# Around the first block's MLP: earlier rows, later weight groups, other buffers for the second down step

## The chip, the cores and the metric

The kernel runs on one core of a Trainium2 chip. Its time is the device time of one execution in microseconds (us), the median of several runs. Engines are named as in the profile: PE (matrix engine), DVE (vector), ACT (scalar), POOL (GpSimd) and SP, whose queue issues the DMAs.

## The reference, cut to what matters

Two transformer blocks run one after the other on 16 sequences of 256 tokens with 512 channels, in fp32. The first block is cross attention to a context, a residual, a layer norm and an MLP with a hidden size of 2048:

```python
out = jnp.einsum('bhnm,bmhd->bnhd', attn, v).reshape(B, N, C)
out = out @ proj_w + proj_b
x = x + out
h = layer_norm(x, n2_w, n2_b)
h = jax.nn.gelu(h @ fc1_w + fc1_b, approximate=False) @ fc2_w + fc2_b
return x + h
```

The second block is causal self attention, cross attention and a small MLP, each with a residual and a layer norm. The change touches the first block's MLP and the end of the attention ahead of it.

## The kernel before, in words

**Precision.** A product of fp32 matrices is made of three matmuls in a faster format: each operand is split into a rounded part and the rest (tiles called `_h` and `_l`, or `x_t` and `c_t`). ACT writes the rounded part, DVE subtracts it to get the rest (`split_lazy`, L141 and L142). POOL does this for the first weights ("early").

**Tiling.** The 4096 rows are 8 batches g of 512 rows (NG = 8, four tiles of 128 rows each). The MLP (class `Mlp0`) runs 32 up steps (fc1 and gelu) and then 32 down steps (fc2): four for each batch, each over two of the eight weight groups of 256 hidden columns. A step is a 2 x 2 block product in seven products instead of eight (a Strassen form): four sums of blocks are made first (`differences`, L802 to L805, for the values, and L851 to L854 in `weigh`, for the weights), and the seven results are added up by DVE. Each product is 12 matmuls of 128 x 128 by 128 x 256, so a step is 84 matmuls.

**Up step** (`up`, PE line L914). Products go in the order 1, 6, 5, 2, 7 with the last two (4, 3) of a step inside the step that follows. `L945` (u2 = p1 + the bank of product 6) and `L970` (u3 = p1 + the bank after product 7) must have read the PSUM bank called "sc" before PE may go on in it. Gelu is on ACT (L979). The gelu'd tile `ho` is stored to DRAM (`hid`, L953). Weights of fc1 are loaded by `fetch` (L818), split and combined by `weigh`; two groups m = 2s, 2s + 1 serve step s of every batch. `begin` loads and prepares the first two groups and the first batch's rows while the attention of the last batch is still running; `open` the next two; `run` weighs groups 4 and 5 after the first up step has been recorded, 6 and 7 after the second.

**Entry.** `last` in `phase1` fills PE's gaps in the attention of the last batch: values, the projection of attention outputs with its residual (`residual`: a row of x is loaded at L671, POOL adds a bias at L672, DVE adds the product at L685, and it is stored at L686), and `Mlp0.begin`. `begin` loads 512 rows `xn` (L870), of which DVE takes the statistics (`bn_stats`, L238) and the normalized value (L247). The attention itself uses all engines: scores on PE (L408), their minimum with the mask on DVE (L423), exp on ACT (L433), transposes (L449) that ACT or DVE copies out (L455, L453), products with the values (L468), and the scaling by reciprocals of sums (L627 on DVE, L629 on POOL, L644 on PE, L647, L136 and L137 on DVE).

**Down step** (`down`, PE line L1027). `hidden(n)` loads the stored values of step n (L993, 1 MB), `sums_down(n)` makes their four sums, `write` splits the seven operands into the slots that PE reads, one after each product of the step before. Products go in the order 1, 6, 2, 7, 5, 4, 3. Weights of fc2 are fetched and weighed during the last four up steps, the last two groups (6 and 7) during the first two down steps. After the four steps of a batch, `end` and `finish` add up the results and the residual rows x (loaded at L1039, POOL adds a bias at L1044) on DVE.

**Buffers.** Big tiles share tags with one buffer each: "raw", "x0", "x1", "x2" (1 MB each in the on-chip memory). A tile of a tag waits until the last reader of the one before it is done. Before the change, `hidden` uses "raw" for even steps and "x0" for odd ones, and the sums of every step but the first are in "x2". In the last up steps "x0" holds weights (fetched at L818 for the last steps), and "x2" holds the gelu'd tile of even up steps.

**Order.** PE's order is the order in which the code records it (`tc.manual_schedule` for PE). The order on ACT, DVE, POOL and SP is made by a scheduler of the framework that runs a timing model of its own; each engine then works strictly in that order, waiting on semaphores.

The functions that the change touches, with the line numbers of the profile:

Of the kernel before, what the change touches and what calls it, by code (L numbers as in the profile page):

```python
# [41 lines left out]
def kernel(ctx: ExitStack, tc: tile.TileContext, a, out):  # L42
# [511 lines left out]
    def phase1():  # L554
# [184 lines left out]
        def last():  # L739
            yield from more_values(NG - 1)  # L740
            right.close()
            mlp = w["mlp"] = Mlp0()
            mlp.small = pool, 4
            yield from residual(NG - 2, 1)
            yield from mlp.begin()
            yield from residual(NG - 1, 0)
            xrs = [residual_row(NG - 1, NT)]
            yield from turned(NG * NB)
            top.close()
            xrs.append(residual_row(NG - 1, NT + 1, mlp.open()))  # L750
            yield from residual(NG - 1, 1, xrs)
# [9 lines left out]
    class Mlp0:  # L761
# [163 lines left out]
        def up(self, n, between):  # L925


            s = n % self.NS if n < NG * self.NS else None
            on, after = s is not None, n > 0
            add = nc.vector.tensor_tensor  # L930
            if on:
                self.product_up(n, 1, "mm", True)
                first = self.flat("p1")
                nc.scalar.copy(first, self.banks[n, "mm"])
            else:
                between[0]()
            if after:
                p1, u2, ho = self.open
                self.product_up(n - 1, 4, "sc", False)
                add(ho[:, :, 0, self.W :], p1, self.banks.pop((n - 1, "sc")), ALU.add)  # L940
                self.gelu(n - 1, ho, 0, slice(self.W, N))
            if on:
                self.product_up(n, 6, "sc", True)
                v2 = self.flat("u2")
                add(v2, first, self.banks[n, "sc"], ALU.add)  # L945
            else:
                between[1]()
            if after:
                self.product_up(n - 1, 3, "pt", False)
                add(ho[:, :, 1, : self.W], u2, self.banks.pop((n - 1, "pt")), ALU.add)  # L950
                self.gelu(n - 1, ho, 1, slice(0, N))
                g, q = divmod(n - 1, self.NS)
                nc.sync.dma_start(  # L953
                    out=self.hid[g][q], in_=ho.rearrange("p m c n -> p (m c n)")
                )
            if not on:
                return
            self.product_up(n, 5, "pt", True)
            between[0]()
            self.product_up(n, 2, "mm", False)  # L960
            if n % 2 == 0:
                ho = self.px.tile([P, 2, 2, N], F32, tag="x2", name="ho")
            else:
                ho = self.up_pool.tile([P, 2, 2, N], F32, tag="ho", name="ho", bufs=1)
            x = self.banks.pop((n, "mm"))
            for mm in range(2):
                self.gelu(n, ho, 0, slice(0, self.W), x[:, mm, :], mm)
            self.product_up(n, 7, "sc", False)
            u3 = self.flat("u3")
            add(u3, first, self.banks[n, "sc"], ALU.add)  # L970
            add(ho[:, :, 1, self.W :], u3, self.banks[n, "pt"], ALU.add)
            between[1]()
            self.open = first, v2, ho
# [15 lines left out]

        def hidden(self, n):  # L990
            g, q = self.order(n)
            h = self.raw_tile("x0" if n % 2 else "raw").rearrange("p (m c n) -> p m c n", m=2, c=2)
            nc.sync.dma_start(out=h.rearrange("p m c n -> p (m c n)"), in_=self.hid[g][q])  # L993
            self.h[n] = h

        def sums_down(self, n):
            h = self.h.pop(n)
            b = [[h[:, :, k, ts(t, self.W)] for k in range(2)] for t in range(2)]
            if n == 0:

                s = [self.place("sums") for _ in range(2)]
                two = self.tmp.tile([P, 4, 2 * P], F32, tag="diff", name="sums")
                two = two.rearrange("p (i m) n -> p i m n", m=2)
                s = [x.rearrange("p (m n) -> p m n", m=2) for x in s] + [two[:, i] for i in range(2)]
            else:
                s = self.px.tile([P, 4, 2, self.W], F32, tag="x2", name="sums")
                s = [s[:, i] for i in range(4)]
            self.differences(b[1][0], b[1][1], b[0][0], b[0][1], s, nc.vector, nc.vector)
            self.a = [b[0][0], b[0][1], b[1][1]] + s
# [26 lines left out]
        def residual(self, g):  # L1036
            x = self.px.tile([P, G, C], F32, tag="x1", name="x")
            for t in range(G):
                nc.sync.dma_start(out=x[:, t, :], in_=xd[0][g][ts(t, P), :])  # L1039
            return x  # L1040
# [46 lines left out]
        def begin(self):  # L1087


            self.fetch(1, 0, self.raw_tile("raw"))  # L1090
            xn = self.px.tile([P, G, C], F32, tag="x2", name="xn")
            for t in range(G):
                self.row(0, t, xn[:, t, :])
            self.fetch(1, 1, self.raw_tile("x1"))
            yield 12 * PASS
            for t in range(G):
                self.normal(xn[:, t, :])
                yield 3 * PASS
            for m in range(2):
                self.weigh(1, m, True)  # L1100
                yield 12 * PASS
            for t in range(G):
                yield self.turn(0, t, xn[:, t, :])
            self.sums(True)
            for i in range(7):
                self.write(i, nc.gpsimd)
# [20 lines left out]
        def run(self, early, after_up):  # L1127

            for m in range(self.NM - 1, 3, -1):
                self.open_group(m)  # L1130
            left = ExitStack()
            self.up_pool = sbuf(left, "work2", 1)
            xn = self.xn
            last = NG * self.NS - 1

            def load(g):

                if g > 1:
                    x = self.pool.tile([P, G, C], F32, tag="raw", name="xn")
                    for t in range(G):  # L1140
                        xn[t] = self.row(g, t, x[:, t, :])

            def go(g, t):
                self.turn(g, t, xn.pop(t))
                if g == 1 and t == 0:
                    xn[G - 1] = self.row(g, G - 1, self.place())
                if t == G - 1:
                    self.sums()

            for n in range(last + 1):  # L1150
                g, s = divmod(n, self.NS)
                between = [lambda: None, lambda: None]
                if g + 1 < NG:
                    if s == 0:
                        load(g + 1)
                    elif s <= 2:
                        for t in (2 * s - 2, 2 * s - 1) if g else ():
                            self.normal(xn[t])
                        between = [lambda t=2 * s - 2 + i: go(g + 1, t) for i in range(2)]
                elif s == self.NS - 1:  # L1160
                    self.sums_down(0)
                self.up(n, between)
                if n == 0:
                    self.weigh(1, 4)
                    self.weigh(1, 5)
                    self.fetch(1, 3, self.raw_tile("raw"))
                elif n == 1:
                    self.weigh(1, 6)
                    self.normal(xn[G - 1])
                    self.weigh(1, 7)  # L1170
                if g == NG - 1:

                    if s == 0:
                        self.fetch(2, 0, self.raw_tile("x0"))
                        self.fetch(2, 1, self.raw_tile("x1"))
                        self.hidden(0)
                    else:
                        self.weigh(2, 2 * s - 2)
                        self.weigh(2, 2 * s - 1)
                        if s < 3:  # L1180
                            self.fetch(2, s + 1, self.raw_tile(f"x{s - 1}"))
            self.at = self.next
            self.up(last + 1, [lambda: self.product_down(0, 1), lambda: self.product_down(0, 6)])
            left.close()
            self.b_stack = ExitStack()
            self.b_fc2 = sbuf(self.b_stack, "b_fc2", 1, "right").tile([P, C], F32, name="b_fc2")
            nc.sync.dma_start(out=self.b_fc2, in_=bcast(a["fc2_b"], C))
            self.down(early, after_up)
# [439 lines left out]
```

## Time and profile before

| | us |
|---|---|
| median of 3 runs | 2765.36 (2759.30 to 2766.42) |
| profiled execution | 2762.91 |
| its span from first to last instruction | 2761.2 |
| PE busy | 2657.0 (96%) |
| DVE busy | 2051.9 (74%) |
| ACT busy | 1821.9 (66%) |
| POOL busy | 630.3 (23%) |
| mean granted clock of PE | 0.991 |

In the profile, the first up step's matmuls start at 716.1 us, the last up step's end near 1061, and the down steps last until about 1390. A busy PE is not PE at its peak, as matmuls are pipelined. "Waits" name for each idle time of an engine what ended it; "granted clock" is the share of full speed that the throttle left to PE.

### The profile page before, as it was taken

Reading aid. Unit: us, or ns where it says so; the run is one execution under the profiler, and the core shown is the slowest. Engines: PE = TensorE matmul, PEld = TensorE weight load, DVE = VectorE, ACT = ScalarE, POOL = GpSimd, SP = SyncE. Lnnn points to the kernel's source line nnn. Section 1 sums busy time; section 2 is a strip of 40 time slices with the busy share of each in tenths; the row PEclk is TensorE's granted clock in tenths of the full one; section 3 lists DMA queues with packets and bytes.
Section 4 is the critical chain, followed back from the end, with each engine's and each line's share of the span. In section 5 each row is a group of like instructions: output and inputs, shape, how many; then the busy total and the mean of one; then the engine's idle time right before and its main releaser. Section 6 shows DMA issues by size and latency. Waiting matters only on the chain.

```text
span 2761.2 us, 56625 instructions
## 1 busy us (share of the span) xinstructions
PE 2657.0 (96%) x18970; PEld 2241.7 (81%) x18970; DVE 2051.9 (74%) x5947; ACT 1821.9 (66%) x5286; POOL 630.3 (23%) x696
## 2 busy tenths in 40 slices
PE   6999999999899998999989999999999999999998
PEld 5777777776899998999968777777777777777787
DVE  7766667657955569999957777777777777777887
ACT  4877777777655555444547778786777776777522
POOL 6222212113401100111211111115212221214333
PEclk9999999999999999999999999999999999999999
DMA  6655656656333344443464665667565665655321
GB/s 214 197 183 170 182 171 192 182 164 169 107 123 138 123 150 175 168 157 136 167 225 159 195 197 187 194 190 227 183 196 188 188 194 170 189 174 173 97 91 54
DMA packets 287808, 465.40 MB, mean 169 GB/s; under 512 B 36256, under 2 KB 188320, under 8 KB 279328
## 3 DMA queue, kind: packets, MB, share of 16 engines
q1 hardware_dynamic: 287520, 461.78, 52.0%
q8 instruction: 153, 2.51, 0.4%
q14 instruction: 135, 1.11, 0.1%
HBM read 284.97 MB, written 176.69 MB: 167 GB/s over the span
## 4 chain that ended last, share of the span: by engine, by line
PE 76%; DVE 10%; DMA 4%; ACT 3%; issue 3%; POOL 2%; SPq 1%; POOLq 0%; DVEq 0%; ACTq 0%
PE ps_p L258 18%; PE ps_v L258 14%; PE down L1027 9%; PE ps_pt L449 9%; PE ps_z L468 5%; PE ps_s L408 5%; PE up_sc L914 5%; PE up_pt L914 3%; PE up_mm L914 3%; PE ps_t L277 2%; DVE e L423 1%; ACT e L433 1%; DVE x L252 1%; DMA d<-qk 1%; PE ps_z L1347 1%
## 5 line engine op out<-in xcount | busy, mean ns | idle before, releaser
L433 ACT ACTIVATE e<-e,mn 128x256 f32<-128x256 f32 (+1 forms) x1024 | 487.5, 480 | 71.7 <-DVE mn L423 69.4
L455 ACT COPY pt<-ps_pt 128x512 f32<-128x512 f32 (+1 forms) x696 | 378.3, 546 | 178.5 <-PE ps_pt L449 165.5
L449 PE MATMUL ps_pt<-ident,e 128*128 128x128 f32 x2816 | 436.3, 273 | 15.4 <-DVE lbias L1289 8.8
L449 PEld LDWEIGHTS ps_pt<-ident,e 128*128 128x128 f32 x2816 | 336.3, 140 | 56.3 <-DVE lbias L1289 5.7
L408 PE MATMUL ps_s<-stack 97*128 97x256 f32 (+1 forms) x1536 | 331.8, 297 | 18.8 <-ACT e L433 12.0
L408 PEld LDWEIGHTS ps_s<-stack 97*128 97x128 f32 (+1 forms) x1536 | 269.0, 190 | 78.3 <-ACT e L433 19.2
L433 ACT ACTIVATE e<-ps_s,mn 128x256 f32<-128x256 f32 x512 | 240.9, 483 | 59.2 <-DVE mn L419 44.0
L1356 POOL TENSOR_TENSOR x<-x,zz 128x256 f32<-128x256 f32 x128 | 95.4, 745 | 737.0 <-DVE zz L1349 687.0
L1027 PE MATMUL down<-w_h,c_t 128*128 128x256 f32 x900 | 255.4, 285 | 5.6 <-DVE c_t L142 5.6
L1027 PE MATMUL down<-w_h,x_t 128*128 128x256 f32 x868 | 245.9, 283 | 4.4 <-ACT x_t L141 4.4
L423 DVE CUSTOM_DVE_ANT_0 e<-mb,ps_s 128x256 f32<-128x256 bf16 x512 | 192.7, 415 | 75.4 <-PE ps_s L408 73.8
L1027 PE MATMUL down<-w_l,x_t 128*128 128x256 f32 x868 | 246.2, 284 | 0.0
L242 POOL TENSOR_TENSOR rstd<-rstd,nhalf 128x1 f32<-128x1 f32 x192 | 142.4, 747 | 360.6 <-DVE rstd L241 358.8
L258 PE MATMUL ps_p<-x_t,q_h 128*128 128x512 f32 x640 | 215.4, 417 | 4.2 <-DVE qk L128 2.1
L419 DVE TENSOR_REDUCE mn<-ps_s 128x2 f32<-128x512 f32 x256 | 175.1, 684 | 48.7 <-PE ps_s L408 46.5
L468 PE MATMUL ps_z<-pt,v 128*32 128x256 f32 (+1 forms) x3072 | 202.2, 370 | 7.2 <-DVE pt L453 6.5
L423 DVE CUSTOM_DVE_ANT_0 e<-tri,ps_s 128x128 f32<-128x128 f32 (+1 forms) x512 | 160.2, 346 | 53.6 <-PE ps_s L408 51.3
L433 ACT ACTIVATION_READ_ACCUMULATOR e<-e,mn 128x1 f32 x1024 | 197.5, 193 | 0.0
L1027 PEld LDWEIGHTS down<-w_h,c_t 128*128 128x128 f32 x900 | 171.0, 190 | 7.8 <-DVE c_t L142 7.8
L1027 PEld LDWEIGHTS down<-w_h,x_t 128*128 128x128 f32 x868 | 166.4, 192 | 4.8 <-ACT x_t L141 4.6
L468 PEld LDWEIGHTS ps_z<-pt,v 128*32 128x32 f32 x3072 | 83.5, 109 | 105.8 <-issue 28.0
L1027 PEld LDWEIGHTS down<-w_l,x_t 128*128 128x128 f32 x868 | 165.2, 190 | 0.0
(250 smaller groups left out, 7247.8 us busy)
## 6 DMA issues: line engine op xcount, KB each, us to landing
stack<-d SPq DMA_DIRECT2D x1152, 128.0 KB
d<-qk SPq DMA_DIRECT2D x192, 512.0 KB
hid<-ho SPq DMA_DIRECT2D x32, 1024.0 KB
raw<-hid SPq DMA_DIRECT2D x32, 1024.0 KB
x<-xd SPq DMA_DIRECT2D x128, 256.0 KB
xd<-x SPq DMA_DIRECT2D x96, 256.0 KB
xin<-in_x_dram SPq DMA_DIRECT2D x32, 256.0 KB
xin<-in_ctx_dram SPq DMA_DIRECT2D x32, 256.0 KB
```

Source lines behind the costliest of these rows:

```text
L242: nc.gpsimd.tensor_tensor(out=rstd[:, 1:2], in0=rstd[:, 0:1], in1=nhalf, op=ALU.pow)
L258: nc.tensor.matmul(ps, w[p], x[q], start=(k == 0 and i == 0), stop=(k == kc - 1 and i == 2))
L408: nc.tensor.matmul(ps[:, t, :], u.st[: self.rows, 0, j, ts(t, P)], u.st[: self.rows, 1, j, :], start=True, stop=True,)
L419: nc.vector.tensor_reduce(mn, ps, AX.X, ALU.min)
L423: nc.vector.tensor_tensor_reduce(out=e[:, at], in0=bias[t], in1=ps[:, t, : job.width[t]], scale=-SC, scalar=BIG, op0=ALU.add, op1=ALU.min, ...
L433: nc.scalar.activation(e[:, at], ps[:, t, :] if bias is None else e[:, at], AF.Exp, bias=mn[:, t : t + 1], scale=-1.0, accum_out=u.rs[:, t ...
L449: nc.tensor.transpose(pp[:, ts(x, P)], e[:, at : at + P], ident)
L455: nc.scalar.copy(pt[:, :n], pp[:, :n])
L468: nc.tensor.matmul(z[ts(j, D), w[0] * P :], job.v[u.i * NT + mc][:, u.c * P + j * D : u.c * P + (j + 1) * D], u.pt[j][:, x0 * P : (x0 + le ...
L914: nc.tensor.matmul(ps[:, mm, :], w[p][:, k, :], x[q][:, k, :], start=(first and mm == k == j == 0), stop=(k == 1 and j == 2), skip_group_c ...
L1027: nc.tensor.matmul(ps[:, t, :], x[p][:, mm, ts(t, P)], w[r][:, bo, :], start=(q == mm == t == j == 0), stop=(q == self.NS - 1 and mm == 1 ...
L1356: nc.gpsimd.tensor_tensor(out=xv, in0=xv, in1=zz, op=ALU.add)
```

## The change

Four edits:

- In `begin`, the four row loads `xn` are recorded ahead of the first weight load `fetch(1, 0)`. In `last`, the first two residual rows of the last batch are asked for ahead of `mlp.begin()`.
- In `run`, the instructions of `weigh(1, 4)` and `weigh(1, 5)` (the third pair of groups) that run on DVE are queued on DVE behind the latest `L945` add, which is that of the first up step (`tc.issue_after` orders the issue and adds no wait).
- `hidden(1)`, the values of the second down step, goes to tag "x2" instead of "x0".
- The sums of that step go to "x0" instead of "x2".

```diff
             mlp.small = pool, 4
             yield from residual(NG - 2, 1)
+            xrs = [residual_row(NG - 1, t) for t in range(NT)]
             yield from mlp.begin()
-            yield from residual(NG - 1, 0)
+            yield from residual(NG - 1, 0, xrs)
...
                 v2 = self.flat("u2")
-                add(v2, first, self.banks[n, "sc"], ALU.add)
+                self.latest = add(v2, first, self.banks[n, "sc"], ALU.add).ins
...
-            h = self.raw_tile("x0" if n % 2 else "raw").rearrange("p (m c n) -> p m c n", m=2, c=2)
+
+            tag = "x2" if n == 1 else "x0" if n % 2 else "raw"
+            h = self.raw_tile(tag).rearrange("p (m c n) -> p m c n", m=2, c=2)
...
-                s = self.px.tile([P, 4, 2, self.W], F32, tag="x2", name="sums")
+                tag = "x0" if n == 1 else "x2"
+                s = self.px.tile([P, 4, 2, self.W], F32, tag=tag, name="sums")
...
-            self.fetch(1, 0, self.raw_tile("raw"))
             xn = self.px.tile([P, G, C], F32, tag="x2", name="xn")
             for t in range(G):
                 self.row(0, t, xn[:, t, :])
+            self.fetch(1, 0, self.raw_tile("raw"))
             self.fetch(1, 1, self.raw_tile("x1"))
...
                 if n == 0:
-                    self.weigh(1, 4)
-                    self.weigh(1, 5)
+                    with tc.issue_after(self.latest):
+                        self.weigh(1, 4)
+                        self.weigh(1, 5)
                     self.fetch(1, 3, self.raw_tile("raw"))
```

In the built programs, PE's instructions stand in the same order. On the other engines the order differs in three stretches, around the entry, the first two up steps, and the first two down steps, and in a few pairs of neighbours elsewhere.

## The prediction

> **What bounds the kernel now.** I read the page first, then PE's waits around the two places that the diff touches, the chain through the first of them, the busy time by stretches, and DVE's timeline.
>
> ```profile
> PE 2657.0 (96%) x18970; PEld 2241.7 (81%) x18970; DVE 2051.9 (74%) x5947; ACT 1821.9 (66%) x5286; POOL 630.3 (23%) x696
> ```
>
> TensorE is busy for 96% of the span, so only time in which it stands still, or runs slowly, can be won. The order of its instructions is the same in both programs, matmul by matmul; the change moves work on the other queues alone. PE's waits in 640 to 770 us (entry to the MLP and first up steps), and in 1030 to 1100 us (last up step, first down steps):
>
> ```profile
> PE ps_z L468 <- DVE pt L453: 6.5, 4, 2.5
> PE up_sc L914 <- DVE u L945: 2.9, 1, 2.9
> ```
>
> ```profile
> PE down L1027 <- ACT x_t L141: 4.4, 1, 4.4
> PE down L1027 <- DVE c_t L142: 2.8, 2, 1.6
> ```
>
> These are the three targets: a 2.5 us stall at 661 (**A**), 2.9 us at 725 (**B**), and 4.4 + 2.8 = 7.2 us at 1065 to 1076 (**C**). The chain through A, with the shorter pieces left out, starts at a load of rows and ends in the stalled matmuls:
>
> ```profile
> 651.89 6.11 DMA xn<-xd
> ...
> 661.29 1.79 PE ps_z L468 x10
> ```
>
> Busy time in stretches (columns: PE, PEld, DVE, ACT, POOL, then the granted clock):
>
> ```profile
> 655.00:660.00 5.00, 3.75 (x27) 2.67 (x25) 2.40 (x7) 2.20 (x8) 5.00 (x9) 1.00 1.03 341
> 660.00:665.00 5.00, 3.71 (x17) 2.20 (x17) 4.24 (x13) 2.06 (x8) 2.48 (x4) 0.66 1.07 236
> ...
> 720.00:725.00 5.00, 2.11 (x18) 1.91 (x16) 5.00 (x13) 2.33 (x4) 0.55 (x1) 1.00 0.28 105
> 725.00:730.00 5.00, 4.97 (x28) 4.84 (x29) 5.00 (x13) 1.38 (x2) 0.55 (x1) 0.66 0.00 0
> ```
>
> ```profile
> 1060.00:1070.00 10.00, 5.61 (x43) 5.11 (x41) 7.02 (x13) 4.71 (x7) 0.00 (x0) 0.88 0.79 292
> 1070.00:1080.00 10.00, 7.22 (x48) 6.92 (x48) 10.00 (x18) 4.77 (x8) 0.00 (x0) 0.78 0.34 128
> 1080.00:1090.00 10.00, 10.00 (x86) 10.00 (x85) 9.93 (x10) 4.25 (x7) 6.84 (x4) 1.00 0.31 97
> 1090.00:1100.00 10.00, 10.00 (x86) 10.00 (x85) 9.93 (x17) 5.06 (x9) 0.00 (x0) 1.00 0.51 199
> 1100.00:1110.00 10.00, 10.00 (x86) 10.00 (x85) 10.00 (x18) 3.73 (x6) 0.00 (x0) 1.00 0.29 106
> 1110.00:1120.00 10.00, 9.78 (x81) 9.54 (x80) 8.76 (x14) 6.48 (x15) 1.70 (x1) 1.00 0.64 240
> ```
>
> Two things are to be seen. After each stall the clock falls: 0.66 over 5 us is 1.7 us of lost time, so A is worth up to 2.5 + 1.7 = 4.2 us and B 2.9 + 1.7 = 4.6. For C, PE issued 43 + 48 matmuls in 20 us where it otherwise issues 86 in 10: 81 are missing, 81 x 10/86 = 9.4 us. All three together are 18.2 us. But DVE is as full as PE: 5.00 of 5 around B, and from 1070 on 9.9 to 10.0 of 10. Whoever removes a stall of PE there brings it sooner to a DVE that is no earlier. So I count what idle time of DVE each edit removes.
>
> **The change part by part.** No arithmetic is added; the number of instructions is the same on every engine. Each queue's new order is read from the built program.
>
> **A, rows ahead of weights.** On SP's queue the four loads of xn (256 KB each) now stand in front of the two of the first weights (512 KB each). The row took 6.11 us with that 1 MB ahead of it; the rows above and the stretch before (254 and 341 GB/s) give 3.1 to 4.1 us for 1 MB, so alone it needs 2.0 to 3.0 us. It is issued where the weight load was, at 650.3, and lands at 652.3 to 653.3; I take the late end, as two stack loads are still in front. The scheduler moves the first bn_stats up too: it now stands in front of the reciprocal L627 and of two pairs of L423, at 651.1 instead of 658.0. DVE waits there from 651.1 to 653.3, of which 1.6 us was idle before as well (L627 waited that long for ACT's exponentials). The old idle of 2.06 us at 656 to 658 goes, 0.6 comes: DVE gains 1.4 us. POOL's early weight groups start some 3 us later, behind which its residual adds queue; POOL is busy for 16.7 of the 30 us from 660 to 690, so I count this at nothing (without that cover, up to 3 us). What is late next is DVE's own backlog: PE's other waits from 664 to 716 sum to about 9 us, nearly all on DVE or ACT, and DVE is at 4.0 to 5.0 of 5 there. So A gives 1.4 us; bounds: 4.2 gained, or 1.7 lost if the row takes 6.1 us again (656.4: DVE idles 5.3 - 1.6 - 2.06 more). Of the two residual rows that are now asked for ahead of the MLP's start, one moves ahead of four stack loads on SP; the wait for them is not on PE's list, so this costs nothing.
>
> **B, third weight groups behind the first step's sums.** DVE before:
>
> ```profile
> 723.97 0.41 DVE L852 TENSOR_TENSOR diff<-raw,diff 128x256 f32<-128x256 f32 x1
> 724.30 0.67 DVE L945 TENSOR_TENSOR u<-p,up_sc 128x512 f32<-128x512 f32 x1
> ...
> 728.63 0.66 DVE L970 TENSOR_TENSOR u<-p,up_sc 128x512 f32<-128x512 f32 x1
> ```
>
> Five subtractions of the third groups (two L851, two L853, one L852) ran ahead of the add L945 that frees PE's bank. They now stand behind it: 5 x 0.34 (start to start) = 1.7 us, so PE's stall shrinks from 2.9 to 1.2 and the clock would probably stay up. But PE's next hold is L970, which frees the same bank for product 4 of this step: it ended at 729.29 and PE took that product at 729.5, so it was already just in time. Only one L854 (0.33) has moved from ahead of it to behind it. Then L970 of the following step ends at 740.7, PE goes on at 740.9, and again one L854 has moved. So PE's 3.4 us are spent waiting for the next add, and B keeps about 0.4 us. Bounds: 0 and 4.6. The groups are needed by the third step, near 746, and end near 733: no cost.
>
> **C, other places for the values and sums.** The values of down step 1 go to x2 instead of x0, the sums to x0. x2 is free once the store issued at 1051.03 has landed, x0 only after the weights' last read at 1060.6. SP now issues the load ahead of the last up step's store, not behind it. Before, it was issued at 1061.62 and landed at 1068.5; now it is there when ACT ends its gelu, near 1061.2. DVE's idle time goes:
>
> ```profile
> 1062.70 1.23 DVE L142 TENSOR_TENSOR w_l<-diff,w_h 128x1024 fp32r<-128x1024 f32 x1 [1.11 <-ACT w_h L141]
> ...
> 1066.63 1.23 DVE L142 TENSOR_TENSOR w_l<-diff,w_h 128x1024 fp32r<-128x1024 f32 x1 [1.11 <-ACT w_h L141]
> 1068.55 0.69 DVE L802 TENSOR_TENSOR sums<-raw 128x512 f32<-128x512 f32 x1 [0.69 <-DMA raw<-hid]
> ```
>
> Together 2.9 of the 2.98 idle in that stretch. In the new order ten operations of 0.60 and one of 1.11 stand from about 1061.7 (with 0.5 of waits for ACT) to the write that product 6 needs: 1069.3. PE has ended product 1 at 1064.8 + 12 x 0.117 = 1066.2, so about 3 us of stall stay and step 2 starts 6 to 7 us sooner. Then it is given back: from 1070 to 1110 DVE had only 0.14 us idle. I laid the new orders of DVE, ACT and SP end to end with the durations of these rows: PE catches DVE up in step 4, near 1113, where finishing the first batch falls on DVE, waits about 3.3 us for a cast of sums, and its lead falls to 2.7 us. That agrees with the idle time that could be removed (2.9). From there PE and DVE go in step as before. So C gives 2.7; bounds 0.5 (two more DVE operations that meet the POOL adds L1044, each 1.78 instead of 0.68) and 9.4. In SP's order the rows for finish are now loaded behind the next values, some 4 us later; they are used 20 us after that, so this costs nothing.
>
> **Sum.** 1.4 + 0.4 + 2.7 = 4.5 us. The profiled execution took 2762.9 us (span 2761.2); it would take 2758.4. It lay 2.45 us below the median of the three runs, so on the median's scale I forecast 2765.4 - 4.5 = 2760.9.
>
> **A rule against the rows.** The rows show the clock falling after stalls of 2.5 and 2.9 us. The Trainium skill (TensorE: Matmul & The Clock Gate, section Why this matters for your kernels) asks for no idle gaps beyond about 3 us and would have left the clock up after both. By that rule A and B could bring at most 2.5 and 2.9 us, and the first rival below would come to 14.8 instead of 18.2 us; the trace disagrees, and the forecast needs neither.
>
> **The rivals.** *The stalls go for good* (20%): DVE yields more than its idle time, for instance because operations that POOL had stretched no longer meet it, and PE keeps its lead. The 6.8 of C with 4 from A and B is 10.8 us, everything 18.2: 2747 to 2755. For it: ACT has half its time free. Against it: 9.9 of 10 on DVE. *The head of DVE blocks* (10%), slower: the row lands late (the three rows behind the first, and two stacks in front), and bn_stats now holds the scores' L423 and the reciprocal behind it. It decides from a landing after 654.7 (651.1 + 1.6 + 2.06). At 656.4 it costs 1.7 on DVE, another 1.7 of clock, and POOL's weights, 3 us later, delay the first up step: +6 us, with C lost too 2771. For it: the 6.11 us; against: the weights that made most of it. *Nothing changes* (12%): A and C only move the wait, +-1 us.
>
> **How the numbers follow.** The forecast has 58%, gains of 1 to 8 us. About 0.3%, 8.3 us, is what a measurement can tell here from no change. Faster by more: the first rival and a little of the forecast's edge, 0.21. Slower by more: the second rival at its worst, 0.08. The rest, 0.71, lies within. The range takes in A's loss with the runs' own spread (7 us) upwards, and most of the first rival downwards: 2753 to 2768.
>
> **What would show it.** A: DVE's bn_stats starts near 653, no 2 us idle at 656 and no 0.66 after 660. B: the stall at L945 near 1 us, and a new wait for L970. C: no wait for raw<-hid, a stall of 2 to 3 us in step 1, then a new one of about 3 us near 1110, and DVE at 10.0 of 10 all the way between. If step 5 begins over 5 us sooner, counted from the start of the last up step, DVE was not the bound and the forecast is wrong.

## The result, and the profile after

The changed kernel took 2755.58 us (median of 7 runs, 2751.17 to 2756.94), the one before 2765.36 (7 runs, 2759.30 to 2767.84). The ratio is 0.9965, 95% interval 0.9952 to 0.9978: 9.8 us faster, with an interval from 6.1 to 13.3 us. The forecast was 2760.9 us, a gain of 4.5. A second comparison on another chip (label e9_after_again below) gave 0.9963 (0.9949 to 0.9976). The profiled execution of after took 2751.17 us, its span is 2749.5 us.

```profile
PE 2654.9 (97%) x18970; PEld 2240.7 (81%) x18970; DVE 2047.4 (74%) x5947; ACT 1820.8 (66%) x5286; POOL 631.4 (23%) x696
```

PE's waits of after, first from 640 to 770 us, then from 1030 to 1130 us (engine, line, releaser; us in all, times, longest):

```profile
PE ps_z L468 <- DVE pt L453: 3.9, 4, 2.3
PE ps_z L468 <- DVE zs L647: 2.5, 1, 2.5
PE up_sc L915 <- DVE u L971: 2.1, 2, 1.8
...
PE down L1031 <- DVE c_t L142: 2.7, 2, 2.5
PE down L1031 <- ACT x_t L141: 0.7, 1, 0.7
```

The stall of 2.5 us at 661 (A) is gone, but two others have come near 700 us. In the first up step PE no longer waits for the add that B clears the way for (L945 of before, L946 here); it waits 1.8 us for the next one (L970 of before, L971 here). In the down steps the 4.4 us for values of the second step are gone; 2.5 us at product 6 stay, and 0.7 us near 1109. The stretches that answer to those of before (length, then PE, PEld, DVE, ACT, POOL with instructions, then the granted clock):

```profile
655.00:660.00 5.00, 4.79 (x34) 3.12 (x35) 5.00 (x19) 3.85 (x13) 3.12 (x6) 1.00 1.08 354
...
700.00:705.00 5.00, 2.31 (x16) 0.70 (x16) 3.80 (x5) 0.00 (x0) 5.00 (x5) 0.67 0.05 19
705.00:710.00 5.00, 5.00 (x16) 3.89 (x16) 2.48 (x7) 3.49 (x7) 2.52 (x3) 0.64 0.76 241
...
725.00:730.00 5.00, 4.11 (x34) 4.11 (x35) 5.00 (x11) 2.48 (x3) 1.68 (x2) 1.00 0.48 157
```

```profile
1060.00:1070.00 10.00, 7.50 (x52) 7.30 (x51) 10.00 (x19) 3.57 (x7) 0.00 (x0) 0.85 0.29 88
1070.00:1080.00 10.00, 10.00 (x84) 10.00 (x84) 9.68 (x17) 5.80 (x9) 0.00 (x0) 0.98 0.54 198
...
1100.00:1110.00 10.00, 9.03 (x74) 8.62 (x73) 10.00 (x18) 6.30 (x15) 0.00 (x0) 1.00 0.57 211
```

The clock's dip at 660 has moved to 700 to 710 (0.67 and 0.64), the one at 725 is gone, the one after the down steps' stall is shorter.

**Reading it by stages.** PE runs the same 18970 matmuls in the same order in every program here. So one can take four matmuls (which before reaches at 654.8, 766.2, 1057.9 and 1134.0 us) and see in each profile how long it took from one to the next; a fifth, at 710.8 us, splits the first stage. This tells far finer than the total time what a place costs, as long as one profile is not taken for the mean. Times of a matmul in the text below are those of before, unless another program is named. The letters are the edits that a program has:

| program | 655 to 711 | 711 to 766 | 655 to 766 | 766 to 1058 | 1058 to 1134 |
|---|---|---|---|---|---|
| before | 55.96 | 55.45 | 111.41 | 291.70 | 76.03 |
| B | 56.66 | 54.86 | 111.53 | 291.70 | 79.14 |
| C | 56.76 | 53.97 | 110.74 | 291.61 | 71.61 |
| B, C | 55.02 | 55.83 | 110.85 | 291.75 | 71.72 |
| A | 55.81 | 52.84 | 108.65 | 292.51 | 77.13 |
| A, C | 56.65 | 52.80 | 109.45 | 292.19 | 71.73 |
| A, B, C (after) | 56.68 | 52.44 | 109.13 | 291.98 | 71.71 |
| A, B, C again | 56.62 | 52.32 | 108.94 | 291.99 | 71.74 |

### The profile page after: what moved, and what is told of

It reads as the page before. It is cut to its first block, busy times and chain, and to the rows that moved or that the text cites. A ratio compares the mean times of both kernels' runs of the same rounds, so it can differ in the third digit from the quotient of the medians.

```text
span 2749.5 us, 56627 instructions
## 1 busy us (share of the span) xinstructions
PE 2654.9 (97%) x18970; PEld 2240.7 (81%) x18970; DVE 2047.4 (74%) x5947; ACT 1820.8 (66%) x5286; POOL 631.4 (23%) x696
## 4 chain that ended last, share of the span: by engine, by line
PE 76%; DVE 12%; DMA 4%; issue 3%; ACT 3%; POOL 2%; SPq 1%; POOLq 0%; DVEq 0%; ACTq 0%
PE ps_p L258 18%; PE ps_v L258 14%; PE down L1031 9%; PE ps_pt L449 9%; PE ps_s L408 6%; PE ps_z L468 5%; PE up_sc L915 5%; PE up_pt L915 3%; PE up_mm L915 3%; PE ps_t L277 2%; DVE e L423 1%; DMA d<-qk 1%; DVE st L238 1%; DVE x L252 1%; ACT e L433 1%
```

## The experiments

Theory 1 is the forecast's: VectorE (DVE) is as full as TensorE (PE) at the three places, and a stall of PE that is taken away is given back at the next one; only idle time of DVE counts. Theory 2: each stall stands for itself and its removal stays won. Under both lies the question of which edit brings what.

### One edit at a time

The kernel before with A alone, B alone, C alone, and with B and C; the edits are those of the diff.

> Edit A alone (rows ahead of weights, residual rows asked for earlier). Two theories. Given back: the profile of after was 5.0 us ahead of before at 684 us and 0.3 us behind at 711 us (both counted from the same matmul at 655), so A alone gains 0 +- 1.5 us in all; in its profile PE is 4 to 6 us ahead after the 668 to 684 us of the attention's end, and loses it again in two stalls of 2 to 2.5 us near 700 with the granted clock at 0.65. Forecast: a gain of 1.4 us with no new stall near 700. Rival, kept: the gain of 4 to 5 us stays, because the losses near 711 in the profile of after came from edit B's order; then the time is 4 to 5 us lower.

> Edit B alone (third weight groups behind the first step's add L945). Forecast: the wait for L945 shrinks from 2.9 to about 1.2 us, the next one for L970 grows, gain 0.4 us. Additive theory: B alone gains the 2.7 us that the profile of after shows between the matmul at 722 us of before and the one at 743. Interaction theory: in the profile of after VectorE reached L945 earlier by 3.9 us and not 1.7 because its weight subtractions no longer ran beside GpSimd's casts (0.42 instead of 1.51 us each), which is A's doing; B alone then leaves a wait of about 1 us and gains 0 to 1 us.

> Edit C alone (values of the second down step in x2, sums in x0). Forecast: step 2 starts 6 to 7 us sooner, a stall of about 3 us comes near 1113 us, gain 2.7 us. Additive theory: the 4.3 us that the profile of after shows between the matmuls at 1058 and 1134 us of before, with a stall under 1 us near 1110. If VectorE were no bound, the gain would be 6.5 us or more and no stall would follow.

> The change without A. Additive theory: 2.7 + 4.3 = 7.0 us faster than before, as far as the whole change is in the sum of its stages, so no slower than the whole change by more than about 1 us. Interaction theory: B without A gives under 1 us, so 4.5 to 5 us faster than before. Forecast: 0.4 + 2.7 = 3.1 us faster. Rival: A keeps its gain in the whole change and this is 4 us or more slower than the whole change.

Measured against before on the same chip (2763.15 us): A alone 2759.95 us, ratio 0.9992 (0.9983 to 1.0); B alone 2764.99, 1.001 (1.0001 to 1.0019); C alone 2757.15, 0.9978 (0.9968 to 0.9989); B and C 2758.09, 0.9979 (0.9970 to 0.9988). So most of the gain is C's; A's interval reaches 1, and B's leaves it out narrowly, on the slow side.

For A the words "given back" hold up to 711 us: 55.81, no better than the four programs without it (55.02 to 56.76). PE was 5.4 us ahead at 684 us, and lost it in two stalls of 2.0 and 2.3 us near 700 and a clock at half speed for 6.8 us. But then the stretch from 711 to 766 us is 1.1 to 3.0 us shorter than in the programs without A, which neither the theory that A is all given back nor the rival had. For B the wait only changed its place, as forecast:

```profile
PE up_sc L914 <- DVE u L970: 2.5, 1, 2.5
...
PE up_sc L914 <- DVE u L945: 0.4, 1, 0.4
```

The 2.7 us that I had read in the profile of after as B's are not there in B alone (from 711 to 743 us it takes 0.6 us less than before, and B with C 0.4 more); they came with A. For C the stall at product 6 is 2.50 us and the later one 0.73 + 0.24 in each of the programs that have it. Without C, though, the wait differs between programs whose instructions stand in the same order there. In B alone the load of the values was issued at 1061.15 by an SP instruction of 1.90 us, and landed 8.6 us after its issue began, where before's, of 0.35 us, landed after 6.9 (SP's timeline of before, SP's of B alone, and DVE's of B alone):

```profile
1061.62 0.35 SPq L993 DMA_DIRECT2D raw<-hid  x1
```

```profile
1061.15 1.90 SPq L993 DMA_DIRECT2D raw<-hid  x1
```

```profile
1069.73 0.69 DVE L802 TENSOR_TENSOR sums<-raw 128x512 f32<-128x512 f32 x1 [2.34 <-DMA raw<-hid]
```

PE's stall there was 6.03 us (5.48 in A alone), against the 4.39 of the one profile that the forecast was made from.

### The change without B, and third groups further back

The first is before with A and C; in the second the `issue_after` names the add after product 7:

```diff
-                self.latest = add(v2, first, self.banks[n, "sc"], ALU.add).ins
+                add(v2, first, self.banks[n, "sc"], ALU.add)
...
-            add(u3, first, self.banks[n, "sc"], ALU.add)
+            self.latest = add(u3, first, self.banks[n, "sc"], ALU.add).ins
```

> The change without B. If B brings its forecast 0.4 us, this stands within 1 us of the whole change (9 to 10 us faster than before), and in the first up step the wait for L945 is back at about 0.7 us with that for L970 near 1.2, as in the kernel with A alone. If B brings the 2.7 us seen between the matmuls at 722 and 743 us in the profile of the whole change, this is 2 to 3 us slower than the whole change. If B costs what it seemed to cost alone (2.8 us slower in the medians), this is the fastest so far.

> As the whole change, but the third weight groups are queued behind L970 (the add after product 7) and not behind L945. Theory that L970 is the next hold: of the 5.7 us between L945 and L970 on VectorE in the profile of the whole change about 3.9 us belong to the third groups, so PE's wait of 1.8 us for L970 goes and the clock with it, 1.8 to 3 us faster than the whole change in the first up step. Theory that VectorE's total work sets the pace: the work moves to the next step, whose adds come later by up to 3.9 us, and the gain is under 0.5 us. Rival, slower: the groups come too late for the third up step near 738 us, a stall of 2 us or more there.

Measured: ratios to before 0.9969 (0.9958 to 0.9981) and 0.9968 (0.9956 to 0.9979), neither to be told from the whole change. In the table A and C without B lose 0.4 us from 711 to 766 and 0.2 from 766 to 1058 against the whole change: this is B's worth beside A. With the third groups behind L970, PE's wait for L970 is gone, and this is what stands in its place (from 715 to 775 us):

```profile
PE up_sc L915 <- DVE rstd L241: 0.7, 1, 0.7
PE up_pt L915 <- DVE ho L972: 0.6, 1, 0.6
PE ps_t L883 <- DVE xn L247: 0.2, 1, 0.2
```

Up to 743 us the program was 1.4 us faster than after, from there to 766 us 1.4 us slower (27.39 and 25.07 us against 28.80 and 23.64). The gain was given back within 25 us, as theory 1 has it.

### Second groups behind the last scaling

```diff
+                scaled[0] = split_sb(u.zs, (z_t[0][:, u.c, :], z_t[1][:, u.c, :]))
...
-            self.weigh(1, 2)
-            self.weigh(1, 3)
+            with tc.issue_after(scaled[0]):
+                self.weigh(1, 2)
+                self.weigh(1, 3)
```

> The whole change, with the second weight groups (four subtractions each on VectorE, 1.5 us each beside GpSimd's casts) queued behind the last scaling of the attention instead of ahead of it. Theory: these subtractions are what turns A's lead of 5 us into stalls of 2.5 and 2.3 us near 700 with a low clock; behind the scaling the stalls shrink to under 2 us together and the first up step starts 3 to 5 us sooner; some of it comes back as a wait in the first two up steps since 6.8 us of VectorE's work moved there: net gain 1 to 3 us over the whole change. Rival: VectorE is the bound, all of it comes back, 0 +- 1 us. Rival, slower: the second up step waits for its weights, 2 us or more lost.

Measured: 0.9971 (0.9961 to 0.9982). The two stalls near 700 are gone and the matmul at 711 us comes 6.9 us sooner than in after (49.77 instead of 56.68 us). From 711 to 766 us it then takes 59.23 instead of 52.44. Both together 109.00, after had 109.13. The new waits from 690 to 770 us (lines are shifted by 2):

```profile
PE up_mm L917 <- DVE xr L687: 3.0, 1, 3.0
PE up_sc L917 <- DVE u L973: 2.2, 1, 2.2
```

All of it came back, as the rival without gain had it. My own guess of 1 to 3 us was wrong.

### One write earlier in the down steps

The last subtraction of weight group 5 is queued behind the write for product 6; the scheduler then also let some other weight work of that stretch change places with writes.

```diff
+                        rest = self.write(self.OPS[i][0])
+                        if n == 0 and i == 6:
+                            d, h, l = self.kept
+                            with tc.issue_after(rest):
+                                nc.vector.tensor_tensor(out=l, in0=d, in1=h.bitcast(F32), op=ALU.subtract)
```

> The whole change, with one 1.2 us operation of VectorE (the rest of the third part of weight group 5 of fc2) queued behind the write for product 6 of the second down step, which it stood ahead of. If VectorE's work is the bound of this stage, as forecast: the stall of 2.50 us at product 6 shrinks to 1.0 to 1.5 us, the ones near 1109 us (0.73 + 0.24) grow by about as much, and the matmul at 1134 us of before comes at the same time +- 0.5 us. If each stall stands for itself: 1.1 us and the clock's 1.7 us stay gained, 2 to 3 us.

Measured: 0.9977 (0.9965 to 0.9989). PE's waits from 1030 to 1130 us:

```profile
PE down L1033 <- ACT x_t L141: 2.6, 1, 2.6
PE down L1033 <- DVE c_t L142: 2.1, 2, 1.4
PE down L1033 <- DVE w_l L142: 0.6, 1, 0.6
```

The first stall shrank from 2.50 to 1.37 us, as expected. But those near 1109 grew from 0.97 to 3.30, and from 1058 to 1134 us it took 74.06 instead of 71.71. More was given back than had been won: up to the matmul at 1122 us DVE idled 1.1 us more and its work took 1.2 us longer in the new order. This stall could not be moved away for good; the equal exchange that I expected did not come.

### Early writes and sums on DVE

```diff
-                self.write(i, nc.gpsimd)
+                self.write(i)
```

and, in the second of the two, the four early sums as well:

```diff
-            own = nc.gpsimd if early else nc.vector
-            self.differences(b[1][0], b[1][1], b[0][0], b[0][1], out, own)
+            own = nc.vector
+            self.differences(b[1][0], b[1][1], b[0][0], b[0][1], out, own, *([own] if early else []))
```

> The whole change once more, beside the two that follow on one chip. Expected: 9 to 10 us faster than before as in the first runs; from the first matmul at 655 us of before to the one at 767 it takes 108 to 109 us (four programs without A: 110.7 to 111.5), from the one at 1058 to 1134 it takes 71.7 (three programs without C: 76.0 to 79.1).

> The whole change, with the seven early subtractions c_t of the first up step (512 columns each, L142) on VectorE and not on GpSimd. Counted as in the forecast, by VectorE's own instructions: 7 x 0.60 = 4.2 us more on an engine that has no idle time there, so the stretch from 655 to 767 us grows by up to 4 us. Theory that the stretched operations are what counts: in the profile of the whole change VectorE loses 10.4 us there in 17 operations that run 2 to 4 times as long while GpSimd is busy; these casts are 9.7 us of GpSimd's time, in which VectorE then no longer slows down; it gets back about 0.7 of each us that overlaps, 3 to 7 us, against 4.2 spent: 0 to 3 us faster, with the stall of 2.5 us near 700 smaller.

> As the run before, and the four early sums of values (512 columns each, 1.27 to 1.46 us on GpSimd) on VectorE too, 4 x 0.60 = 2.4 us more there. By VectorE's own instructions 2.4 us slower than the run before, 6.6 us slower than the whole change. By the stretched operations: 5.5 us of GpSimd's time less beside VectorE, 0 to 1.5 us faster than the run before.

Measured against before (2770.26 us on this chip): the whole change again 2760.81; writes on DVE 2759.13, 0.9958 (0.9945 to 0.9972); writes and sums on DVE 2755.94, 0.9948 (0.9935 to 0.9962). From 655 to 766 us: 108.94, 108.51 and 104.78. So the writes alone bring nothing to speak of, and the 4.2 us more of DVE's work cost nothing either, where counting DVE's own instructions, as the forecast did, had up to 4 us. The stalls near 700 did not shrink: 2.55 + 1.87 us became one of 4.38. DVE's stretched time stayed at 10.2 us (9.9 in the whole change again; counted is what an operation that took over one and a half times the median of its shape took above that median, and every one of them ran beside an operation of POOL), as its operations now met what was left on POOL. With the sums moved too it fell to 5.3 us, and the stage is 4.2 us shorter although DVE has 11 x 0.60 = 6.6 us more of its own to do. This is more than either count had expected. Its busy time in the stage is what it was (98.2 us, and 98.1 in the whole change again); its idle time fell from 10.8 to 6.6 us, and PE's stalls from 12.6 to 9.0. How much of the gain is the stretch and how much the waits for POOL's chain, these runs don't part. This is the same subtraction in the whole change, and then in the last program:

```profile
695.16 1.48 DVE L852 TENSOR_TENSOR diff<-raw 128x256 f32<-128x256 f32 x1 [1.18 <-POOL w_l L142]
696.56 1.50 DVE L854 TENSOR_TENSOR diff<-raw 128x256 f32<-128x256 f32 x1
```

```profile
697.53 0.42 DVE L852 TENSOR_TENSOR diff<-raw 128x256 f32<-128x256 f32 x1
697.86 0.42 DVE L854 TENSOR_TENSOR diff<-raw 128x256 f32<-128x256 f32 x1
```

By its ratio to before this last program is the fastest of all here, 4.9 us below the whole change in the medians of 6 runs each; the runs of the two overlap (2752.97 to 2760.61 against 2756.05 to 2763.63).

### Without POOL's adds in the first batch

```diff
-                elif q == 3 and g < NG - 1:
+                elif q == 3 and 0 < g < NG - 1:
```

> The whole change without GpSimd's four adds L1044 in the first batch (the bias of fc2 is left out of its rows). In the profile of the whole change four of VectorE's writes there take 1.78 instead of 0.68 us. Theory that VectorE sets the pace of the first down steps: 4.4 us of it come free after the stall at product 6, so the stalls of 0.73 and 0.24 us near 1109 go, the one of 2.50 near 1066 stays: 1.0 us less between the matmuls at 1058 and 1134 us of before, not 4.4, since TensorE has no more to win there. Rival: the stalls near 1109 stay because ScalarE's cast is what they wait for: no difference.

This kernel leaves the bias of fc2 out of the first batch's rows. Measured: 70.79 us from 1058 to 1134 instead of 71.74, 0.95 us less where 1.0 was expected (in the total, 0.9969 with 0.9953 to 0.9985, it can't be seen). DVE had 4.0 us less work there, and used it for 3.1 us more of idle time. The stall of 2.50 us stayed, the 0.73 went, 0.24 remained. So DVE is the bound as far as PE's next stall, and no further.

## Why the prediction was right in direction, and half the size

The time fell inside the range, and the sign was right; the gain was 4.5 us where 9.8 were measured (6.1 at the least by the interval). Point by point:

**That a stall taken away is given back.** Shown three times: third groups further back, second groups further back and the write moved forward each took a stall of PE away, or half of it, and brought no time. So the first rival, stalls that go for good because PE keeps its lead, is wrong in that, though its time of 2747 to 2755 us lay nearer to the measured 2755.6 than the forecast's 2760.9. The instance that it gave, operations of DVE that POOL no longer stretches, fits what was measured for A (below).

**That DVE's work sets the pace.** Right in the down steps. Work plus idle time is the length of any stretch, so the sum proves nothing by itself; what counts is which of the two changed. From the matmul at 1058 to the one at 1122 us they are 59.63 + 4.40 before, 59.63 + 5.50 with A, 59.88 + 7.26 with B, and with C 59.2 + 0.4 to 0.5 in five programs: the work stayed to 0.7 us, and the idle time went almost whole. From 655 to 766 us it is only part of the truth. DVE idles there for 11 to 13 us in the eight profiles of the table, and 4.2 and 6.6 us more of its work did not lengthen the stage when POOL had less to do. There DVE and POOL set the pace together, and a count of DVE's instructions at their usual length misses it.

**C.** Forecast 2.7, measured 4.3 against the profiled execution and 5.7 against the mean of the three programs without it (77.43 less 71.70). The term is right in kind and was mis-sized twice. First, I closed the window at 1110 us and counted 2.9 us of idle time; up to the matmul at 1122, just behind the point where PE caught DVE up, it was 4.40, of which 0.5 stayed. The row 1110 to 1120 of the prediction shows most of what was left out: DVE is busy for 8.76 of its 10 us. The later stall that I laid end to end at 3.3 us measured 0.97. Second, I took the one profile as the usual case: its load landed 6.9 us after its issue, where others took 8.0 and 8.6 us. The edit takes the load out of the path, so it also wins what a bad landing costs.

**A.** Forecast 1.4, measured 2.0 from 655 to 766 us (108.65 and 109.45 against 111.41 and 110.74, without B), of which 0.7 is lost again by 1058: 1.3 net. That this is so near the forecast is in part luck. The row took 3.60 us alone, where 2.0 to 3.0 were estimated, and the first bn_stats waited:

```profile
652.68 0.70 DVE L238 BATCH_NORM_STATS2 st<-xn 128x6 f32<-128x512 f32 x1 [2.73 <-DMA xn<-xd]
```

Before, that wait was 2.06 us, and 1.27 to 2.01 in the three other programs without A. By this wait alone nothing was won. But it now covers the waits that DVE had around it, as the forecast had it: from the matmul at 640 to the one at 668 us, DVE's idle time in all was 7.7 to 9.5 us in the four programs without A and 5.8 to 6.8 in the four with it, on average 2.1 less (forecast: 1.4). This did not stay. From 640 to 766 us DVE idled 17.8 us on average without A and 17.5 with it, so 1.8 of the 2.1 came back as other waits; its busy time, for the same 299 instructions, fell from 108.2 to 106.4. And the stall of 2.54 us that A was aimed at was 0.9 to 1.4 us in the three other programs without A, with no dip of the clock there. So what is left of A's gain stands in DVE's busy time, and the time by which POOL stretches its operations from 655 to 766, counted as above, was 12.0 to 14.2 us without A and 9.9 to 12.0 with it. That less stretch makes up A's gain is likely by these sums, but no run changes the stretch alone.

I had counted POOL's later weight groups at nothing, and looked for no new stall there. That step failed: on POOL the rest of the second group now stood behind a sum that waits for ACT,

```profile
691.33 1.29 POOL L805 TENSOR_TENSOR sums<-xt 128x512 f32<-128x512 f32 x1 [3.04 <-ACT xt L889]
692.56 2.56 POOL L142 TENSOR_TENSOR w_l<-diff,w_h 128x1024 fp32r<-128x1024 f32 x1
695.08 1.27 POOL L803 TENSOR_TENSOR sums<-xt 128x512 f32<-128x512 f32 x1
696.31 1.46 POOL L142 TENSOR_TENSOR c_t<-xt,x_t 128x512 fp32r<-128x512 f32 x1
```

so that DVE's subtraction at 695.16 (above) waited 1.18 us for it, with the scaling L647 queued behind and PE behind that. Of the 2.52 us near 700 this wait explains 1.18; besides, PE was 5.0 us ahead of before at 684 us, and DVE's scaling was not. Stalls of 2.52 + 2.31 us stand there where before had 0.19 + 1.70: 2.9 us more, and the clock at half speed for 6.8 us came on top. That this is close to the 3 us that I had named for POOL is luck. What the step costs in the sum stays open: with the second groups behind the scaling both stalls were gone and the stage took the same 109.0 us, while with less on POOL it took 104.8.

**B.** Forecast 0.4. Beside A it is 0.4 + 0.2 us in the table, alone nothing: right, with the wait for L970 as its reason. B alone was 1 in 1000 slower in the ratio, with an interval of 1.0001 to 1.0019; its profile shows 3.1 us more in 1058 to 1134, where its order is that of before. Whether B brings this about by when it makes load and store meet, or whether it is chance, stays open.

**The slow rival** (bn_stats blocks DVE's head) did not happen: it needed a landing after 654.7 us, the row was there at 652.7.

**What the stages don't hold.** 1.3 for A, 0.6 for B and 5.7 for C are 7.6 us, inside the interval of 6.1 to 13.3, but 2.2 short of its middle. Of the 5.3 us by which the forecast fell short, C holds 3.0, A and B together 0.1, and 2.2 are left over. From 1414 us on, where the order is the same but for neighbours, the profiles of all programs differ by up to 10 us (1333 to 1343 us to the end), so a rest of 2 us can't be placed. The first matmul of the table, too, comes anywhere between 652.4 and 658.2 us in the fourteen profiles.

**The chances.** Faster by more than 0.3% had 0.21; the measured 0.35% and 0.37% lie just over that bound, with intervals that hold it.

## What to carry to other kernels

Where two engines are full, don't add up the stalls of the one: over the stretch in which they run into each other, what can be won is idle time of the other, counted up to the point where the first has caught it up, not to the end of a window. A stall that hangs on a DMA's landing has no single price: look at the same instructions in other runs before taking one profile's number. And if two engines block each other, the work of one at its usual durations is no measure: 6.6 us more for DVE, taken from POOL, made a stage 4.2 us shorter.

## What the runs showed of the hardware

**POOL and DVE.** A subtraction of 128x256 on DVE takes 0.42 us, and 1.48 to 1.50 beside POOL's operations: in after, POOL's sum ran from 695.08 to 696.35 and DVE's L852 ended at 696.64, 0.3 us behind it; POOL's next ended at 697.77 and DVE's L854 at 698.06. In these rows DVE's operation does not end before POOL's is done and most of its own usual duration has passed behind that. The Trainium skill (SBUF — State Buffer, section Who interferes with whom) says that a DVE instruction with two inputs in the on-chip memory contends with a POOL instruction that reads it, and calls the ports that they share an exclusive lock; these rows agree. What I hadn't expected is the sum: 10 to 14 us of DVE's time in some 110, in the eight profiles of the table.

**The clock.** Single stalls of 2.19 us (second groups behind, at 727.9) to 2.58 (C alone, at 676.1) each brought 3.4 us at half speed, and one of 2.99 (second groups behind, at 714.6) no more than that. Below it goes both ways: 1.70 (C alone, at 703.1) and 1.96 us (B alone, at 680.4) brought it, 1.70 (before, at 706.3), 1.95 (before, at 683.6) and 1.81 (after, at 725.9) did not; nor did 1.37 (write moved, at 1065). So the same stall does not have the same price in every run. The traces show what decides. The stretches at half speed begin on a grid of 3.41 us: those of before, at 661.46, 726.32 and 1067.65, lie 19 and 100 such periods apart. From 600 to 1400 us of all fourteen profiles, each of the 34 periods at full speed in which PE idled 1.84 us or more was followed by one at half speed, and none in which it idled 1.70 or less was. So the 1.95 us of before, which straddle two periods with 1.70 in the second, brought nothing, and the 1.96 us of B alone, which lie in one, brought it. Over the whole span the border is less sharp: between 1.57 and 2.01 us it goes both ways. The Trainium skill's rule of about 3 us (TensorE: Matmul & The Clock Gate, section Why this matters for your kernels) is too generous for this kernel by these rows.
